# A state-space scan on one core: carries copied once for three units, delta and x multiplied after the transpose, and one scaling in eight moved to GpSimd

## The chip, the cores and the metric

The kernel runs on one core of one Trainium2 chip. The metric is device time in microseconds, from one execution to the next the median of three: 25196.08 us (25184.54 to 25197.58). A core has five engines that run side by side and meet only at semaphores: PE (TensorE, matrix multiplications and transposes into PSUM), DVE (VectorE), ACT (ScalarE), POOL (GpSimd) and SP, which here only issues DMAs. Each engine works through its own queue in order. An instruction that waits holds up everything behind it on its engine, and nothing elsewhere, unless something elsewhere needs it.

## What is computed

Two layers on 8 images of 64 x 64 tokens and 192 channels, in fp32. The change lies in the second, a selective scan in four directions `k` (rows, columns, and both backwards) over 384 inner channels and 16 states per channel:

```
xs     = silu(conv3x3(in_proj(x)))                 # in four orders of the tokens
dts, B, C = x_proj(xs);   delta = softplus(dt_proj(dts) + bias)
h[t]   = exp(delta[t] * A) * h[t-1] + (delta[t] * xs[t]) * B[t]      # per channel and state
y[t]   = sum over states of h[t] * C[t]
out    = out_proj(layernorm(y1 + y2 + y3 + y4 + xs*D) * silu(z)) + x
```

## The kernel before, in words

`layer1` handles one image after another. For each there are two parts. First a stage that I call the front: a planner (`Flow`) interleaves `front` (projection, 3x3 convolution and silu of image b, with its results stored in DRAM twice, by rows in `xo[0]` and by columns in `xo[1]`), `prologue` (what the first stretch of the scan needs) and `finish` (layer norm, gate and output projection of image b-1). The planner is a list of generators: each yields a step with its engine and an estimated cost, or takes and gives a slot of a pool; the step that can start first comes next. What it picks becomes a fixed order of instructions on each engine. Then comes `main`, the scan, whose order is written out by hand.

The scan of an image has 32 steps (4 directions x 8 stretches of 512 tokens). A step has 24 units: 8 pairs `p` of states times 3 groups `d` of 128 channels. A unit holds 2 halves `f` of 64 channels x 2 states on the 128 partitions, 512 tokens wide. For unit u, `main` emits in this order:

- `run(u)`: two `tensor_tensor_scan` on DVE (L1561), one for each half, then on POOL the copy of the last column to `cy`, the carry into the next step (L1573), and the product `hc` of h and C (L1575)
- `decay(u + 2)`: two exponentials on ACT (`ea`, L1534)
- `weigh`, 3, 3 and 2 times in the three units of a pair: on ACT, delta times x, laid out by tokens (`duT`), is scaled by a column of B (`pw`, L1519). Eight of these, 4 blocks `j` of tokens x 2 states `i`, make the input of one pair. The list `todo` runs ten ahead: the eighth scaling of pair p+1, (j=3, i=1), is emitted in the middle unit, 3p+1, of pair p
- `supply(u + 1)`: eight transposes on PE turn `pw` into `g` (L1545), the additive input of the scan, in PSUM with two buffers
- `collect(u - 1)`: PE sums `hc` over the states into `y` (L1590); `add(u - 2)`, for the last pair alone, adds y to the accumulator on DVE (L1601, L1599)
- one piece of `prepare(s + 1)`, from a table: loading xc, `project`, `keep`, `turn_b`, `step`, `soft` (three activations), `delta` on DVE (L1447), `times_u` (delta times x, on POOL, L1454), `turn` (PE, L1460), `keep_du` (copies the transposed product from PSUM to `duT`, DVE, L1467)

So the queues read: PE `supply(u+1), collect(u-1), supply(u+2), collect(u)`; POOL `cy(u), hc(u), cy(u+1), hc(u+1)`. Pools that matter: `hs` and `hc` 3 buffers each, `g` 2, `ea` 3, `pw` 8 tiles (two pairs).

Of the kernel before, what the change touches and what calls it, by code (L numbers as in the profile page):

```python
# [8 lines left out]
F32 = mybir.dt.float32  # L9
# [985 lines left out]
def layer1(tc, consts, x1s, mv1, out, w_in, w_x, w_dt, w_out):  # L995
# [7 lines left out]
    with ExitStack() as ctx:  # L1003
# [47 lines left out]
        nc.vector.tensor_copy(gb.rearrange("p m b -> p (m b)"), pb[:, : 2 * DT * nb])  # L1051

        wxz = [wp.tile([CP, CT, DIN], F32, name=f"wi1{n}") for n in "xz"]

        keeper = []
        o = lambda ins: keeper[-1](ins)

        def scaled(f, b, half):

            for ct in range(CT):  # L1060
                r = yield step(
                    "ACT",
                    0.6,
                    lambda: [
                        nc.scalar.activation(
                            wxz[half][:, ct],
                            wi[:, ct, half * DIN : half * DIN + DIN],
                            AF.Copy,
                            scale=sc[:, b * CT + ct : b * CT + ct + 1],
                        )  # L1070
                    ],
                )
            return r

        def front(f, cx, mq, b, xo):

            fp = cx.enter_context(tc.tile_pool(name="fr1", bufs=1, reuse_waits="tile"))
            pads = [fp.tile([128, HI + 2, WI + 2], F32, name=f"pad{i}") for i in range(2)]
            for tag, n in (("xl", 3), ("fx", 2), ("pad", 2), ("xs", 2), ("xt", 1)):
                f.pool(tag, n)  # L1080
            got = {}

            def load():
                for d in range(DT):
                    for t in range(NT):
                        tk = slice(t * TT, t * TT + TT)
                        yield "take", "xl"
                        xl = got["xl", d, t] = fp.tile([CP, CT, TT], F32, name="xl1", bufs=3)
                        r = yield step("SP", 0.1, lambda: [nc.sync.dma_start(out=xl, in_=image(x1s[b])[:, :, tk])])
                        f.at["xl", d, t] = r + 3  # L1090

            def project():
                yield from scaled(f, b, 0)
                for d in range(DT):
                    for t in range(NT):
                        yield "wait", ("xl", d, t)
                        xl = got["xl", d, t]
                        yield "take", "fx"
                        ps = got["ps", d, t] = mq.tile([128, TT], F32, name="p_x1", tag="fx", bufs=2)
                        r = f.at["ps", d, t] = yield step(  # L1100
                            "PE",
                            1.9,
                            lambda: [
                                nc.tensor.matmul(
                                    ps, wxz[0][:, ct, d * 128 : d * 128 + 128], xl[:, ct], start=ct == 0, stop=ct == 1
                                )
                                for ct in range(CT)
                            ],
                        )
                        f.give("xl", r)  # L1110
# [61 lines left out]
            def store():  # L1172
                for d in range(DT):
                    yield "wait", ("conv", d)
                    xs = got["xs", d]
                    for h in range(2):
# [11 lines left out]
                            r,  # L1188
                        )
                    yield "take", "xt"  # L1190
                    xt = fp.tile([128, WI, HI], F32, name="xt1")
                    r = yield step("ACT", 7.2, lambda: [nc.scalar.copy(xt, xs.rearrange("p h w -> p w h"))])
                    f.give("xs", r + 5)
                    r = yield step(
                        "SP", 0.1, lambda: [nc.sync.dma_start(out=xo[1][:, d], in_=xt.rearrange("p w h -> p (w h)"))], r
                    )
                    f.give("xt", r + 10)
                f.at["front"] = r

            return [convolve(), fill(), project(), load(), store()]  # L1200

        def finish(f, cx, mq, b):

            fp = cx.enter_context(tc.tile_pool(name="fi1", bufs=1, side="right", reuse_waits="tile"))
            full = [128, DT, TT]
            for tag, n in (("sq", 1), ("rs", 2), ("z", 2), ("xl2", 3)):
                f.pool(tag, n)
# [72 lines left out]
            def gate():  # L1280
                yield from scaled(f, b, 1)
                for t in range(NT):
                    yield "wait", ("xl2", t)
                    xl = got["xl2", t]
                    for d in range(DT):
# [6 lines left out]
                                nc.tensor.matmul(  # L1292
                                    ps, wxz[1][:, ct, d * 128 : d * 128 + 128], xl[:, ct], start=ct == 0, stop=ct == 1
                                )
# [71 lines left out]
        def scan(xo):  # L1366
# [18 lines left out]
            def prepare(s, bank=lambda name: mp.tile([128, TT], F32, name=name, tag="mm")):  # L1385
# [5 lines left out]
                def load():  # L1391
                    st["xc"] = pools["pr1"].tile([128, DT, TT], F32, name="xc")
                    o(nc.sync.dma_start(out=st["xc"], in_=xo[k % 2][:, :, c * TT : c * TT + TT]))
                    if first(s):
                        st["wd"] = pools["pr1"].tile([45, DIN], F32, name="wd")
# [55 lines left out]

                def times_u(d):
                    st["du", d] = pools["pr1"].tile([128, TT], F32, name="du", tag="tmp")
                    o(nc.gpsimd.tensor_mul(st["du", d], st["de", d], st["xc"][:, d]))  # L1454

                def turn(d):
                    st["p_du", d] = pt = bank("p_du")
                    for j in range(NB1):
                        o(
                            nc.tensor.transpose(  # L1460
                                pt[:, j * 128 : j * 128 + 128], st["du", d][:, j * 128 : j * 128 + 128], ident
                            )
                        )

                def keep_du(d):
                    o(
                        nc.vector.tensor_copy(  # L1467
                            st["duT"][:, :, d * 128 : d * 128 + 128],
                            st["p_du", d].rearrange("p (j t) -> p j t", j=NB1),
                        )  # L1470
                    )
# [10 lines left out]
                    9: [(delta, 0), (step, 1)],  # L1482
                    10: [(soft, 1), (times_u, 0)],
                    11: [(delta, 1), (turn, 0), (repeat_delta, s, 0)],
                    12: [(keep_du, 0), (step, 2), (times_u, 1)],
                    13: [(soft, 2)],
                    14: [(delta, 2), (turn, 1)],
                    15: [(keep_du, 1), (times_u, 2)],
                    16: [(turn, 2)],
# [22 lines left out]
            def weigh(s, p, j, i):  # L1512

                st = state[s]
                if i == 0:
                    st["pw", p, j] = pools["pw1"].tile([128, 2 * DT, 2, 64], F32, name="pw")
                n = 2 * p + i
                o(
                    nc.scalar.activation(  # L1519
                        st["pw", p, j][:, :, i],  # L1520
                        st["duT"][:, j].rearrange("p (g c) -> p g c", c=64),
                        AF.Copy,
                        scale=st["bt"][:, j, n : n + 1],
                    )
                )

# [25 lines left out]
            def run(u):  # L1552
# [3 lines left out]
                ea, g = made.pop(("e", u)), made.pop(("g", u))  # L1556
                h = pools["h1"].tile([128, 2, TT], F32, name="hs")
                rev = (lambda ap: ap) if k < 2 else (lambda ap: ap[:, ::-1])
                for f in range(2):
# [9 lines left out]
                    )  # L1569
                if "cy" not in st:  # L1570
                    st["cy"] = pools["pr1"].tile([128, NP1, DT, 2], F32, name="cy")
                last = TT - 1 if k < 2 else 0
                o(nc.gpsimd.tensor_copy(st["cy"][:, p, d], h[:, :, last]))  # L1573
                made["hc", u] = hc = pools["h1"].tile([128, 2, TT], F32, name="hc")
                o(nc.gpsimd.tensor_mul(hc, h, bc(st["cb", p], 1, [128, 2, TT])))  # L1575

            def collect(u):
# [30 lines left out]
            def prologue(f, mq, front_pools):  # L1608

                yield "wait", "front"  # L1610
                front_pools.close()
                for name, n in (("pr1", 2), ("dr1", 4), ("pw1", 8), ("bc1", 3), ("e1", 3)):
                    spool(name, n)
# [18 lines left out]
                for t in todo[:10]:  # L1632
                    yield step("ACT", 0.55, lambda: weigh(*t), f.free["ACT"])
                for u in range(2):
                    yield step("ACT", 1.35, lambda: decay(u), None, "explog")

            def prologue_of(f, d):
# [9 lines left out]
                yield step("SP", 0.1, lambda: repeat_delta(0, d), r)  # L1647
                yield "take", "tmp"
                r = yield step("POOL", 1.3, lambda: ready["times_u"](d), r)
                yield "take", "mm"  # L1650
                r = yield step("PE", 0.6, lambda: ready["turn"](d))
                f.give("tmp", r)
                yield "wait", "bt"
# [4 lines left out]
            def main():  # L1658
                for name, n, kw in (("h1", 3, {}), ("y1", 1, dict(space=PSUM)), ("g1", 2, dict(space=PSUM))):
                    spool(name, n, **kw)  # L1660
                supply(0)
                rest = iter(todo[10:])
# [32 lines left out]
        for b in range(nb + 1):  # L1695
# [8 lines left out]
            if b < nb:  # L1704
                xo = [ddp.tile([128, DT, L], F32, name=f"xo{i}") for i in range(2)]
                chains += front(f, fr_x, mq, b, xo)
                prologue, main = scan(xo)
# [112 lines left out]
```

## Time and profile before

| | us |
|---|---|
| median of three runs | 25196.08 |
| the profiled execution | 25213.53 |
| its span, first to last instruction | 25211.5 |
| layer 0, up to the first `hc` | 5863.9 |
| one image's scan, first to last of 768 `hc` (8297.7 to 10486.4) | 2188.7 |
| one front between two scans (last `hc` 8055.9 to first `hc` 8297.7) | 241.8 |

The profiled execution lies 17 us above the median. Times in the timeline count from the start of the span. A group's mean is the duration of one instruction; two of the same engine can overlap by a little, so what counts for the rate is the distance from start to start.

### The profile page before, as it was taken

Reading aid. Unit: us, or ns where it says so; the run is one execution under the profiler, and the core shown is the slowest. Engines: PE = TensorE matmul, PEld = TensorE weight load, DVE = VectorE, ACT = ScalarE, POOL = GpSimd, SP = SyncE. Lnnn points to the kernel's source line nnn. Section 1 sums busy time; section 2 is a strip of 40 time slices with the busy share of each in tenths; the row PEclk is TensorE's granted clock in tenths of the full one; section 3 lists DMA queues with packets and bytes.
Section 4 is the critical chain, followed back from the end, with each engine's and each line's share of the span. In section 5 each row is a group of like instructions: output and inputs, shape, how many; then the busy total and the mean of one; then the engine's idle time right before and its main releaser. Section 6 shows DMA issues by size and latency. Waiting matters only on the chain.

```text
span 25211.5 us, 312991 instructions
## 1 busy us (share of the span) xinstructions
PE 21347.4 (85%) x100012; PEld 10381.6 (41%) x100012; DVE 21583.5 (86%) x22090; ACT 21653.2 (86%) x38251; POOL 16862.8 (67%) x13639
## 2 busy tenths in 40 slices
PE   7888888887888888888888888888888888888888
PEld 3444444443443444344434443444344434443444
DVE  6777667658999899899989998999899989988998
ACT  5666566558998999899989998999899989998998
POOL 0111111116997799599959995999599959986997
PEclk7888888888999999999999999999999999999999
DMA  1111111112222222222222222222222222222222
GB/s 45 38 36 42 37 37 42 33 28 88 66 66 76 78 65 69 85 68 65 66 88 66 66 66 87 66 66 69 85 67 67 64 89 65 67 66 87 66 66 59
DMA packets 1129703, 1608.06 MB, mean 64 GB/s; under 512 B 259360, under 2 KB 458432, under 8 KB 1118848
## 3 DMA queue, kind: packets, MB, share of 16 engines
q1 hardware_dynamic: 1128064, 1588.03, 22.4%
q8 instruction: 806, 13.21, 0.2%
q14 instruction: 833, 6.82, 0.1%
HBM read 1024.65 MB, written 160.17 MB: 47 GB/s over the span
## 4 chain that ended last, share of the span: by engine, by line
POOL 55%; PE 23%; issue 9%; DVE 6%; ACT 4%; DMA 3%; SPq 1%; POOLq 0%; DVEq 0%; ACTq 0%
POOL hc L1575 49%; POOL cy L1573 4%; DVE xs L1165 3%; PE p_f L937 2%; PE y L1590 2%; PE p_x L429 2%; PE p_f L957 2%; PE p_z L512 2%; POOL du L1454 1%; DMA xc<-xo 1%; PE p_y L771 1%; DVE xs L325 1%; PE p_o L854 1%; PE p_o L1339 1%; PE p_y L768 1%
## 5 line engine op out<-in xcount | busy, mean ns | idle before, releaser
L1575 POOL TENSOR_TENSOR hc<-hs,cb 128x1024 f32<-128x1024 f32 x6144 | 14582.9, 2374 | 10.4 <-POOL cy L1573 6.1
L1561 DVE TENSOR_TENSOR_SCAN hs<-ea,cy,g 128x512 f32<-128x512 f32 x10752 | 13058.6, 1263 | 787.6 <-PE g L1545 425.4
L1519 ACT ACTIVATE pw<-duT,bt 128x384 f32<-128x384 f32 x16384 | 8873.2, 601 | 12.8 <-DVE duT L1467 12.8
L1590 PE MATMUL y<-hc,sel 128*64 128x512 f32 x24576 | 6655.0, 620 | 2467.4 <-POOL hc L1575 2461.7
L1534 ACT ACTIVATE ea<-dr,an 128x512 f32<-128x512 f32 x12288 | 8125.5, 709 | 348.9 <-DVE hs L1561 326.2
L1545 PEld LDWEIGHTS g<-ident,pw 128*128 128x128 f32 x49152 | 5306.8, 141 | 4303.0 <-issue 2670.4
L1545 PE MATMUL g<-ident,pw 128*128 128x128 f32 x49152 | 6773.8, 280 | 30.6 <-DVE hs L1561 12.9
L1590 PEld LDWEIGHTS y<-hc,sel 128*64 128x64 f32 x24576 | 1228.9, 135 | 3886.9 <-POOL hc L1575 3627.0
L1573 POOL COPY cy<-hs 128x2 f32<-128x2 f32 x6144 | 1165.1, 190 | 1547.2 <-DVE hs L1561 1482.2
L1454 POOL TENSOR_TENSOR du<-de,xc 128x512 f32<-128x512 f32 x768 | 983.4, 1280 | 1639.2 <-DVE de L1447 1621.1
L1561 DVE TENSOR_TENSOR_SCAN hs<-ea,g 128x512 f32<-128x512 f32 x1536 | 1776.9, 1204 | 178.1 <-PE g L1545 122.7
L346 POOL TENSOR_TENSOR s<-x 96x512 f32<-96x512 f32 x64 | 88.5, 1383 | 2366.9 <-DVE x L325 2169.7
L346 POOL TENSOR_TENSOR s<-sq 96x512 f32<-96x512 f32 x128 | 221.2, 1728 | 1049.2 <-ACT sq L359 909.8
L1433 PE MATMUL p_dt<-xdbl,wd 13*128 13x512 f32 x1536 | 857.3, 639 | 41.4 <-DVE de L1447 39.5
L1165 DVE SCALAR_TENSOR_TENSOR xs<-pad,p,xs 128x4096 f32<-128x4096 f32 x192 | 860.8, 4484 | 36.9 <-ACT xs L1155 29.7
L1404 PE MATMUL p_d<-xc,wx 128*44 128x512 f32 x1536 | 792.1, 598 | 96.3 <-DMA xc<-xo 96.3
L937 PE MATMUL p_f<-h,wf 96*128 96x512 f32 x1536 | 786.4, 656 | 4.8 <-ACT m L913 3.3
L325 DVE SCALAR_TENSOR_TENSOR x<-xx,p,x 96x512 f32<-96x512 f32 x1024 | 720.2, 744 | 29.3 <-ACT x L314 29.1
L1447 DVE SCALAR_TENSOR_TENSOR de<-p_dt,spa 128x512 f32<-128x512 f32 x768 | 524.0, 682 | 255.6 <-ACT spa L1442 253.4
L325 DVE SCALAR_TENSOR_TENSOR xs<-xin,p,xs 96x512 f32<-96x512 f32 x1024 | 702.0, 755 | 17.2 <-ACT xs L314 17.2
L957 PE MATMUL p_f<-m,wf 128*96 128x512 f32 x1536 | 711.3, 614 | 0.8 <-ACT m L913 0.8
L1601 DVE TENSOR_TENSOR yacc<-yacc,y 128x512 f32<-128x512 f32 x576 | 624.6, 1084 | 18.5 <-PE y L1590 18.5
(199 smaller groups left out, 20330.1 us busy)
## 6 DMA issues: line engine op xcount, KB each, us to landing
cb<-cd SPq DMA_DIRECT2D x4096, 128.0 KB
dr<-de SPq DMA_DIRECT2D x3072, 128.0 KB
xc<-xo SPq DMA_DIRECT2D x256, 768.0 KB
e<-csd SPq DMA_DIRECT2D x256, 384.0 KB
xl<-x SPq DMA_DIRECT2D x256, 384.0 KB
xo<-xs SPq DMA_DIRECT2D x48, 1024.0 KB
xo<-xt SPq DMA_DIRECT2D x24, 2048.0 KB
xl<-in_x SPq DMA_DIRECT2D x64, 384.0 KB
```

The costliest lines, as they stand in the source:

```text
L325: nc.vector.scalar_tensor_tensor(im(out[:, ct]), tap(ct, j), w[:, ct, j : j + 1], im(out[:, ct]), ALU.mult, ALU.add)
L937: nc.tensor.matmul(ps, wf1[:, ct, mt * 128 : mt * 128 + 128], h[:, ct], start=ct == 0, stop=ct == 1)
L957: nc.tensor.matmul(ps[:CP], wf2[:, kt, ct * CP : ct * CP + CP], m[:, kt], start=kt == 0, stop=kt == 5)
L1165: nc.vector.scalar_tensor_tensor(xs, tap(j), kw[:, d, j : j + 1], xs, ALU.mult, ALU.add)
L1454: o(nc.gpsimd.tensor_mul(st["du", d], st["de", d], st["xc"][:, d]))
L1519: nc.scalar.activation(st["pw", p, j][:, :, i], st["duT"][:, j].rearrange("p (g c) -> p g c", c=64), AF.Copy, scale=st["bt"][:, j, n : n + 1],
L1534: nc.scalar.activation(ea[:, f], state[s]["dr", d][:, f], AF.Exp, scale=an[:, k, p, at : at + 1])
L1545: nc.tensor.transpose(g[:, f, j * 128 : j * 128 + 128], state[s]["pw", p, j][:, 2 * d + f].rearrange("p a b -> p (a b)"), ident,)
L1561: nc.vector.tensor_tensor_scan(rev(h[:, f]), rev(ea[:, f]), rev(g[:, f]), 0.0 if first(s) else state[s - 1]["cy"][:, p, d, f : f + 1], ALU ...
L1573: o(nc.gpsimd.tensor_copy(st["cy"][:, p, d], h[:, :, last]))
L1575: o(nc.gpsimd.tensor_mul(hc, h, bc(st["cb", p], 1, [128, 2, TT])))
L1590: o(nc.tensor.matmul(y[half[f]], sel, hc[:, f], start=p == 0 and k > 0, stop=p == NP1 - 1))
```

## The change

Four edits that belong together:

1. The two `hs` tiles of a unit become one tile for the three units of a pair, with 2 buffers, and the carries of the pair are copied once, after the third `hc`: 8 copies of 128x6 in a step instead of 24 of 128x2. `hc` comes right after the scan, and has 2 buffers instead of 3.
2. `times_u` goes. `turn` transposes delta itself, and `keep_du` multiplies it by x, laid out by tokens (`ut`), on its way out of PSUM. For this the front stores x a third time, by tokens (`by_tokens`: transposes, an ACT copy and a DMA for each of 24 tiles), and each step loads `ut`, by one DMA or, for columns, two.
3. The eighth scaling of each pair, (j=3, i=1), runs on POOL.
4. To make room: the scaled projection weights move into the front's and the finish's own pools, `xl` has 2 buffers instead of 3, and the `ea` pool opens in `main`, so that `decay(0)` and `decay(1)` are emitted there and not in the planned part.

```diff
             def front(...):
+            wx_b = fp.tile([CP, CT, DIN], F32, name="wx1b")
-            for tag, n in (("xl", 3), ("fx", 2), ("pad", 2), ("xs", 2), ("xt", 1)):
+            for tag, n in (("xl", 2), ("fx", 2), ("pad", 2), ("xs", 2), ("xt", 1), ("xq", 2)):
...
+                        f.fork(by_tokens(d, h, xs, r))
...
+            def by_tokens(d, h, xs, r):
+                xf = xs.rearrange("p h w -> p (h w)")
+                for g in range(h * NT // 2, h * NT // 2 + NT // 2):
+                    yield "take", "fx"
+                    ps = mq.tile([128, TT], F32, name="p_xq", tag="fx", bufs=2)
+                    r = yield step("PE", 0.6, lambda: [nc.tensor.transpose(...) for j in range(NB1)], max(r, f.now))
+                    yield "take", "xq"
+                    xq = fp.tile([128, NB1, 128], F32, name="xq1", bufs=2)
+                    q = yield step("ACT", 0.6, lambda: [nc.scalar.copy(xq.rearrange("p j c -> p (j c)"), ps)], r)
+                    f.give("fx", q)
+                    dst = xo[2][g * TT : g * TT + TT, d * 128 : d * 128 + 128].rearrange("(j p) c -> p j c", p=128)
+                    q = yield step("SP", 0.1, lambda: [nc.sync.dma_start(out=dst, in_=xq)], q)
...
                 def load():
+                    st["ut"] = pools["pr1"].tile([128, NB1, DIN], F32, name="ut", bufs=1)
+                    if k % 2 == 0:
+                        o(nc.sync.dma_start(out=st["ut"], in_=src))
+                    else:
+                        for i in range(2): ...
...
-                def times_u(d):
-                    st["du", d] = pools["pr1"].tile([128, TT], F32, name="du", tag="tmp")
-                    o(nc.gpsimd.tensor_mul(st["du", d], st["de", d], st["xc"][:, d]))
...
                 def keep_du(d):
-                        nc.vector.tensor_copy(
+                        nc.vector.tensor_mul(
                             st["duT"][:, :, d * 128 : d * 128 + 128],
                             st["p_du", d].rearrange("p (j t) -> p j t", j=NB1),
+                            st["ut"][:, :, d * 128 : d * 128 + 128],
...
             def weigh(s, p, j, i):
+                if (j, i) == (NB1 - 1, 1):
+                    o(nc.gpsimd.tensor_scalar_mul(dst, src, scale))
+                else:
+                    o(nc.scalar.activation(dst, src, AF.Copy, scale=scale))
...
             def run(u):
-                h = pools["h1"].tile([128, 2, TT], F32, name="hs")
+                if d == 0:
+                    st["hs"] = pools["h1"].tile([128, DT, 2, TT], F32, name="hs")
+                h = st["hs"][:, d]
...
-                o(nc.gpsimd.tensor_copy(st["cy"][:, p, d], h[:, :, last]))
                 made["hc", u] = hc = pools["h1"].tile([128, 2, TT], F32, name="hc")
                 o(nc.gpsimd.tensor_mul(hc, h, bc(st["cb", p], 1, [128, 2, TT])))
+                if d == DT - 1:
+                    o(nc.gpsimd.tensor_copy(st["cy"][:, p], st["hs"][:, :, :, last]))
...
-                for name, n, kw in (("h1", 3, {}), ("y1", 1, dict(space=PSUM)), ("g1", 2, dict(space=PSUM))):
+                for name, n, kw in (("e1", 3, {}), ("h1", 2, {}), ("y1", 1, dict(space=PSUM)), ("g1", 2, dict(space=PSUM))):
+                decay(0)
+                decay(1)
                 supply(0)
```

More of the change, by code (lines that the diff above doesn't have):

```diff
@@ L1051, in layer1, with scaled @@
         nc.vector.tensor_copy(gb.rearrange("p m b -> p (m b)"), pb[:, : 2 * DT * nb])
-        wxz = [wp.tile([CP, CT, DIN], F32, name=f"wi1{n}") for n in "xz"]
         keeper = []
         o = lambda ins: keeper[-1](ins)
-        def scaled(f, b, half):
+        def scaled(w, b, half):
             for ct in range(CT):
@@ L1065, in scaled @@
                         nc.scalar.activation(
-                            wxz[half][:, ct],
+                            w[:, ct],
                             wi[:, ct, half * DIN : half * DIN + DIN],
@@ L1087, in load @@
                         yield "take", "xl"
-                        xl = got["xl", d, t] = fp.tile([CP, CT, TT], F32, name="xl1", bufs=3)
+                        xl = got["xl", d, t] = fp.tile([CP, CT, TT], F32, name="xl1", bufs=2)
                         r = yield step("SP", 0.1, lambda: [nc.sync.dma_start(out=xl, in_=image(x1s[b])[:, :, tk])])
@@ L1092, in project @@
             def project():
-                yield from scaled(f, b, 0)
+                yield from scaled(wx_b, b, 0)
                 for d in range(DT):
@@ L1104, in project @@
                                 nc.tensor.matmul(
-                                    ps, wxz[0][:, ct, d * 128 : d * 128 + 128], xl[:, ct], start=ct == 0, stop=ct == 1
+                                    ps, wx_b[:, ct, d * 128 : d * 128 + 128], xl[:, ct], start=ct == 0, stop=ct == 1
                                 )
@@ L1192, in store @@
                     r = yield step("ACT", 7.2, lambda: [nc.scalar.copy(xt, xs.rearrange("p h w -> p w h"))])
-                    f.give("xs", r + 5)
+                    if last := f.part(("xs", d), 3, r + 5):
+                        f.give("xs", last)
                     r = yield step(
@@ L1197, in store @@
                     f.give("xt", r + 10)
-                f.at["front"] = r
+                if last := f.part("front", 2 * DT + 1, r):
+                    f.at["front"] = last
+            def by_tokens(d, h, xs, r):
[3 more added lines that the diff above has]
+                    ps = mq.tile([128, TT], F32, name="p_xq", tag="fx", bufs=2)
+                    r = yield step(
+                        "PE",
+                        0.6,
+                        lambda: [
+                            nc.tensor.transpose(
+                                ps[:, j * 128 : j * 128 + 128], xf[:, g * TT + j * 128 : g * TT + j * 128 + 128], ident
+                            )
+                            for j in range(NB1)
+                        ],
+                        max(r, f.now),
+                    )
+                    yield "take", "xq"
[4 more added lines that the diff above has]
+                    q = yield step("SP", 0.1, lambda: [nc.sync.dma_start(out=dst, in_=xq)], q)
+                    f.give("xq", q + 2)
+                if last := f.part(("xs", d), 3, r):
+                    f.give("xs", last)
+                if last := f.part("front", 2 * DT + 1, q):
+                    f.at["front"] = last
             return [convolve(), fill(), project(), load(), store()]
@@ L1205, in finish @@
             full = [128, DT, TT]
+            wz_b = fp.tile([CP, CT, DIN], F32, name="wz1b")
             for tag, n in (("sq", 1), ("rs", 2), ("z", 2), ("xl2", 3)):
@@ L1280, in gate @@
             def gate():
-                yield from scaled(f, b, 1)
+                yield from scaled(wz_b, b, 1)
                 for t in range(NT):
@@ L1292, in gate @@
                                 nc.tensor.matmul(
-                                    ps, wxz[1][:, ct, d * 128 : d * 128 + 128], xl[:, ct], start=ct == 0, stop=ct == 1
+                                    ps, wz_b[:, ct, d * 128 : d * 128 + 128], xl[:, ct], start=ct == 0, stop=ct == 1
                                 )
@@ L1393, in load @@
                     o(nc.sync.dma_start(out=st["xc"], in_=xo[k % 2][:, :, c * TT : c * TT + TT]))
+                    st["ut"] = pools["pr1"].tile([128, NB1, DIN], F32, name="ut", bufs=1)
+                    if k % 2 == 0:
+                        src = xo[2][c * TT : c * TT + TT].rearrange("(j p) m -> p j m", p=128)
+                        o(nc.sync.dma_start(out=st["ut"], in_=src))
+                    else:
+                        for i in range(2):
+                            src = xo[2].rearrange("(h w) m -> w h m", w=WI)[c * RT + i : c * RT + RT : 2]
+                            o(nc.sync.dma_start(out=st["ut"][i * 64 : i * 64 + 64], in_=src.rearrange("j h m -> h j m")))
                     if first(s):
@@ L1460, in turn @@
                             nc.tensor.transpose(
-                                pt[:, j * 128 : j * 128 + 128], st["du", d][:, j * 128 : j * 128 + 128], ident
+                                pt[:, j * 128 : j * 128 + 128], st["de", d][:, j * 128 : j * 128 + 128], ident
                             )
@@ L1482, in prepare @@
                     9: [(delta, 0), (step, 1)],
-                    10: [(soft, 1), (times_u, 0)],
+                    10: [(soft, 1)],
                     11: [(delta, 1), (turn, 0), (repeat_delta, s, 0)],
-                    12: [(keep_du, 0), (step, 2), (times_u, 1)],
+                    12: [(keep_du, 0), (step, 2)],
                     13: [(soft, 2)],
                     14: [(delta, 2), (turn, 1)],
-                    15: [(keep_du, 1), (times_u, 2)],
+                    15: [(keep_du, 1)],
                     16: [(turn, 2)],
@@ L1517, in weigh @@
                 n = 2 * p + i
[L1518 to L1525, printed above, removed]
+                dst, src = st["pw", p, j][:, :, i], st["duT"][:, j].rearrange("p (g c) -> p g c", c=64)
+                scale = st["bt"][:, j, n : n + 1]
+                if (j, i) == (NB1 - 1, 1):
+                    o(nc.gpsimd.tensor_scalar_mul(dst, src, scale))
+                else:
+                    o(nc.scalar.activation(dst, src, AF.Copy, scale=scale))
             def decay(u):
@@ L1569, in run @@
                     )
[L1570 to L1573, printed above, removed]
                 made["hc", u] = hc = pools["h1"].tile([128, 2, TT], F32, name="hc")
                 o(nc.gpsimd.tensor_mul(hc, h, bc(st["cb", p], 1, [128, 2, TT])))
+                if d == DT - 1:
+                    if "cy" not in st:
+                        st["cy"] = pools["pr1"].tile([128, NP1, DT, 2], F32, name="cy")
+                    last = TT - 1 if k < 2 else 0
+                    o(nc.gpsimd.tensor_copy(st["cy"][:, p], st["hs"][:, :, :, last]))
             def collect(u):
@@ L1611, in prologue @@
                 front_pools.close()
-                for name, n in (("pr1", 2), ("dr1", 4), ("pw1", 8), ("bc1", 3), ("e1", 3)):
+                for name, n in (("pr1", 2), ("dr1", 4), ("pw1", 8), ("bc1", 3)):
                     spool(name, n)
@@ L1632, in prologue @@
                 for t in todo[:10]:
-                    yield step("ACT", 0.55, lambda: weigh(*t), f.free["ACT"])
-                for u in range(2):
-                    yield step("ACT", 1.35, lambda: decay(u), None, "explog")
+                    if t[2:] == (NB1 - 1, 1):
+                        yield step("POOL", 0.8, lambda: weigh(*t), 0.0)
+                    else:
+                        yield step("ACT", 0.55, lambda: weigh(*t), f.free["ACT"])
             def prologue_of(f, d):
@@ L1647, in prologue_of @@
                 yield step("SP", 0.1, lambda: repeat_delta(0, d), r)
-                yield "take", "tmp"
-                r = yield step("POOL", 1.3, lambda: ready["times_u"](d), r)
                 yield "take", "mm"
-                r = yield step("PE", 0.6, lambda: ready["turn"](d))
-                f.give("tmp", r)
+                yield step("PE", 0.6, lambda: ready["turn"](d), r)
                 yield "wait", "bt"
@@ L1705, in layer1 @@
                 xo = [ddp.tile([128, DT, L], F32, name=f"xo{i}") for i in range(2)]
+                xo.append(ddp.tile([L, DIN], F32, name="xo2"))
                 chains += front(f, fr_x, mq, b, xo)
```

## The prediction

> **What bounds the kernel now.** I read the page first: the busy shares and the chain of work that ended last.
>
> ```profile
> PE 21347.4 (85%) x100012; PEld 10381.6 (41%) x100012; DVE 21583.5 (86%) x22090; ACT 21653.2 (86%) x38251; POOL 16862.8 (67%) x13639
> ...
> POOL hc L1575 49%; POOL cy L1573 4%; DVE xs L1165 3%; PE p_f L937 2%; PE y L1590 2%; PE p_x L429 2%; PE p_f L957 2%; PE p_z L512 2%; POOL du L1454 1%; DMA xc<-xo 1%; PE p_y L771 1%; DVE xs L325 1%; PE p_o L854 1%; PE p_o L1339 1%; PE p_y L768 1%
> ```
>
> The chain names POOL, and all three POOL instructions that the change removes or thins out stand in it. Shares over a whole span mix stages, so I took the scan of one image alone, cut by direction (columns: PE, PEld, DVE, ACT, POOL, clock, DMA share, GB/s).
>
> ```profile
> 8300.00:8840.00 540.00, 476.42 (x2584) 231.10 (x2584) 497.30 (x464) 529.14 (x953) 498.44 (x403) 1.00 0.24 65
> 8850.00:9390.00 540.00, 452.56 (x2463) 222.53 (x2462) 504.61 (x460) 525.72 (x944) 492.33 (x399) 1.00 0.23 64
> 9400.00:9940.00 540.00, 461.68 (x2516) 227.01 (x2514) 505.18 (x471) 535.31 (x964) 504.74 (x407) 1.00 0.24 66
> ```
>
> Here ACT is busy 97 to 99% of the time, DVE 92 to 94%, POOL 91 to 93%: three engines in balance. 768 products from 8297.7 to 10486.4 us make 2188.7 / 767 = 2.854 us for a unit, 68.5 us for a step of 24, 8.56 us for a pair of states. Where engines balance, latencies decide, so the third view is the timeline of one image's scan.
>
> ```profile
> 10003.65 0.24 POOL L1573 COPY cy<-hs 128x2 f32<-128x2 f32 x1
> 10003.77 1.61 ACT L1519 ACTIVATE pw<-duT,bt 128x384 f32<-128x384 f32 x3
> ...
> 10004.83 1.38 PE L1545 MATMUL g<-ident,pw 128*128 128x128 f32 x8
> ...
> 10005.43 0.53 PEld L1545 LDWEIGHTS g<-ident,pw 128*128 128x128 f32 x5 [0.30 <-ACT pw L1519]
> ...
> 10014.15 7.12 DVE L1561 TENSOR_TENSOR_SCAN hs<-ea,cy,g 128x512 f32<-128x512 f32 x6
> ```
>
> and, from the step before:
>
> ```profile
> 9760.50 1.09 PE L1545 MATMUL g<-ident,pw 128*128 128x128 f32 x8
> ...
> 9761.73 2.45 DVE L1561 TENSOR_TENSOR_SCAN hs<-ea,cy,g 128x512 f32<-128x512 f32 x2 [1.14 <-PE g L1545]
> ...
> 9764.25 0.19 POOL L1573 COPY cy<-hs 128x2 f32<-128x2 f32 x1 [0.94 <-DVE hs L1561]
> ```
>
> Four latencies come out of this. The last scaling of a pair ends at 10003.77 + 1.61 = 10005.38; PE had stopped at the fourth block's transpose, does five more and ends at 10004.83 + 1.38 = 10006.21: 0.83 us from scaling to g. g ended at 9761.59 and the scan that waited began at 9761.73: 0.14. That scan ended at 9764.18 and POOL began at 9764.25: 0.07. Six scans in a row take 7.12, so a unit of two takes 2.38 from start to start, 2.45 to its end. The same timeline has an `hc` at 10001.34 and the next POOL instruction at 10003.65: 2.31 from start to start.
>
> **What the Trainium skill says.** "GPSIMD Engine Reference", section "Elementwise — side-by-side cycle accounting": an operation with two tensor inputs has a floor of about 2.5 cycles an element, since both reads share a port; its section "Engine selection" says that one-input operations run at roughly line rate. The trace agrees: `hc` has 1024 elements in 2374 ns and `du` 512 in 1280, so 2.14 ns an element and 186 ns fixed, while a copy of 132 elements takes 290 ns and one of 2 takes 190, 0.8 ns an element.
>
> ```profile
> L877 POOL COPY xx<-xx x56: 284/290/7972, 236.8 to 5534.7; 96x132 f32<-96x132 f32 x56
> ```
>
> "ScalarE: Activation LUTs", section "What ACT_TABLE_LOAD costs": 186 ns plus 93 for a per-partition operand plus 0.833 an element, and neighbours overlap by 93. That is 599 ns for a scaling (the row of L1519 has 601), and three take 1.61, so one more costs 0.505.
>
> **The change part by part, for a step.**
>
> ACT loses 8 of 64 scalings, 8 x 0.505 = 4.0 us. It ran at 97 to 99% of 68.5, so it can do a step in some 63.5 and bounds nothing any more.
>
> POOL loses three `du` (3 x 1.28 = 3.8) and 16 of 24 carry copies (16 x 0.14, the distance 10003.65 to the `hc` behind it, = 2.2), and gains 8 scalings of W each. No row has a per-partition scaling of 128x384 on POOL. From below: the copies' rate, 186 + 384 x 0.8 = 0.49 us; from above: a two-input product, 186 + 384 x 2.14 = 1.01. It reads one tensor, but also a scalar a partition, and writes in six strided rows; I take 0.62, nearer the low end, and keep both for the range. So POOL needs about as much as before (-6.0 + 5.0) and isn't full either.
>
> DVE: `keep_du` becomes a product from PSUM, about 0.69 (the row `xx<-p_o,xs` has 686 ns) instead of 0.67: nothing. By load alone DVE would be the next bound: 24 x 2.38 = 57.1, plus per step three `delta` and three `keep_du` (4.1), `keep` and `keep_b` (0.85) and three adds at 0.67 by rows or 1.28 by columns: 64 to 66 us.
>
> The new wait is what decides. The eighth scaling of pair p+1 is emitted after `run(3p+1)`, so in POOL's queue it stands behind `hc(3p+1)`, which cannot begin before the scan of unit 3p+1 has ended. `supply(3p+3)` needs it for its fourth transpose, and the scan of unit 3p+3 needs all eight. ACT, without that product ahead of it, delivered it early. This makes a loop over one pair: scan 3p+1, its product, the scaling, five transposes, scan 3p+3, and one more scan to 3p+4, where the next round begins:
>
> 2.45 (scan) + 0.07 + 2.31 (hc) + 0.62 (scaling) + 0.83 (PE) + 0.14 + 2.38 (scan 3p+3) = 8.80 us.
>
> Eight pairs: 70.4 a step, already over 68.5. Behind the waiting transpose stand `collect(3p+1)` and `supply(3p+4)` on PE; by the loop's times these end 1.09 + 1.0 after the fifth transpose, in time for scan 3p+4 (2.38 after 3p+3), except where a piece lies between: `project(0)` in unit 2 (1.02) costs 0.7 once a step, and in the first direction the skip matmuls another 1.1. DVE's extra work hides in the stall when it falls behind scans 3p+1 or 3p+2, since scan 3p+3 waits 1.6 us there; what follows a scan of unit 3p+3 does not: `delta(0)` in unit 9, `keep_du(0)` in 12, `keep_du(1)` in 15, and one add of three, 0.68 + 0.69 + 0.69 + 0.67 to 1.28, on average 3.0. Step: 70.4 + 3.0 + 0.7 + 0.3 (1.1 in a quarter of the steps) = 74.4, against 68.5: +5.9. Times 256 steps: +1510 us.
>
> The other buffers cost nothing by this count: `hc` with 2 needs `collect(u-2)`, which ends before scan u does; `hs` for a pair is asked for again six units later.
>
> Front: 24 ACT copies of a 128x512 bank, at some 0.5 each start to start, and 24 x 4 transposes (0.65 each four, as `p_du` at 10042.90) mostly lie beside the convolution, where DVE is the bound (117 of 120 us busy) and ACT idles half the time. Bare is the tail: after the last silu another 8 copies and 2 MB stored ahead of the load of xc, which took 9.96 us behind the xt store already, while `du` leaves the prologue's chain (1.3). SP issues all of these in order. I take +6 an image, from 0 to 20, in all +50. `decay(0)` and `decay(1)` in `main` are hidden: ACT was free at 8289 and the first scan waited for g until 8295.07. The `ut` loads (768 KB a step, one or two issues) have some 12 units before `keep_du(0)` wants them, and the DMA engines are 24% busy.
>
> Sum, against the profiled execution: 25213.5 + 1510 + 50 = 26774; the median lies 17 lower, and part of today's stalls at pair ends is counted in both sums, so I round down to 26,700.
>
> **Rivals.** (1) Slower, but by POOL's own price: W near 1.0, as a two-input product, adds 0.39 x 2048 pairs = 800: 27,500. For it: the strided output. Against it: the copies. (2) The wait is largely the one that is there already: ACT's scaling comes late today too (g waited for pw 984 us in all), so a pair grows only by 0.2: +410 + 50, 25,650. (3) The other side, faster: the wait does not bind, ACT's 4 us are the gain, and DVE decides with 65 us a step and about 2 of today's stalls, 67: -1.5 x 256, 24,850. For it: ACT's 99%, and a POOL queue shorter by 1 us. It needs the scaling to end within 2.38 - 0.97 = 1.4 us of scan 3p+1's end, where the product in front of it takes 2.31; so it holds only if the scaling did not stand behind that product, or if the scan needed only half of g, and the scan that waited began after the eighth transpose.
>
> **Chances.** The forecast 0.60, rival 1 0.14, rival 2 0.13, rival 3 0.11, no change 0.02. My range, 25,600 to 27,500, takes in rival 2 and the upper price of W and leaves out rival 3 and a little above. A measurement of this kernel tells 0.2% from no change. Slower: 0.60 + 0.14 + 0.13 = 0.87.
>
> **What would show it.** Right: in the waits, PE's weight load of g waiting for POOL's pw, about 1.5 us in 2048 pairs, and DVE's scans waiting for g, far above today's 548; ACT and DVE down to 86 to 88% in the scan; 73 to 75 us a step. The POOL scaling's row gives W. Wrong: ACT or DVE still above 95%, or the scan's wait ending on ea; a front longer than 260 us would put the loss elsewhere.

## The result, and the profile after

The changed kernel takes 29407.43 us (29380.3 to 29446.31) against 25192.64 for the kernel before (four executions each): the ratio is 1.1675, with a 95% interval of 1.1654 to 1.1695. Slower, as forecast, but 2,700 us more than the 26,700 predicted and outside the range. The profiled execution has a span of 29378.6 us. Its page, shares and granted clock of PE:

```profile
PE 23739.5 (81%) x100780; PEld 11405.7 (39%) x100780; DVE 21668.7 (74%) x22090; ACT 21217.7 (72%) x36402; POOL 17927.8 (61%) x10823
...
PEclk7888888898889888988898889888888898889888
...
L1607 POOL TENSOR_TENSOR hc<-hs,cb 128x1024 f32<-128x1024 f32 x6144 | 14535.4, 2369 | 4591.0 <-PE g L1579 1456.1
L1597 DVE TENSOR_TENSOR_SCAN hs<-ea,cy,g 128x512 f32<-128x512 f32 x10752 | 13061.9, 1264 | 4508.9 <-PE g L1579 2619.7
...
L1557 POOL TENSOR_SCALAR pw<-duT,bt 128x384 f32<-128x384 f32 x2048 | 2563.5, 1252 | 1754.6 <-DVE duT L1502 1338.2
```

The same two kinds of line on the page of before:

```profile
PEclk7888888888999999999999999999999999999999
...
L1561 DVE TENSOR_TENSOR_SCAN hs<-ea,cy,g 128x512 f32<-128x512 f32 x10752 | 13058.6, 1263 | 787.6 <-PE g L1545 425.4
```

DVE and ACT do about as many microseconds of work as before, and the products `hc` take no longer; what is new is the idle time in front of the scans, 4508.9 us instead of 787.6. The POOL scaling has a row of its own: 1252 ns. PE's clock line shows mostly 8 in the scan where the page of before has 9. The waits of the changed kernel name the place (us in total, times, longest; PEld is PE's weight load, and `issue` is time in which nothing that the profile shows was waited for):

```profile
ACT ea L1568 <- DVE hs L1597: 4736.8, 3577, 7.0
PEld g L1579 <- POOL pw L1557: 4376.3, 2040, 3.4
PE g L1579 <- POOL pw L1557: 3892.5, 2040, 3.2
PEld g L1579 <- issue: 3689.3, 3560, 2.8
DVE hs L1597 <- PE g L1579: 3077.7, 2646, 3.3
```

PE's transposes wait for POOL's scaling 2040 times; there are 2048 pairs of states. The scans wait for those transposes, and ACT for buffers that the scans free. The same stretch as the windows of before, in the third image:

```profile
9360.00:9900.00 540.00, 427.16 (x1997) 205.60 (x1995) 411.13 (x373) 411.02 (x713) 426.48 (x253) 0.87 0.25 66
```

No engine is above 80% busy, where ACT had 97 to 99. One round of the loop in the timeline, with two bursts of PE work from before and after it:

```profile
7308.80 1.87 PE L1579 MATMUL g<-ident,pw 128*128 128x128 f32 x8
...
7310.70 2.45 DVE L1597 TENSOR_TENSOR_SCAN hs<-ea,cy,g 128x512 f32<-128x512 f32 x2 [0.53 <-PE g L1579]
...
7313.33 2.37 POOL L1607 TENSOR_TENSOR hc<-hs,cb 128x1024 f32<-128x1024 f32 x1 [1.14 <-DVE hs L1597]
...
7313.68 1.08 PE L1627 MATMUL y<-hc,sel 128*64 128x512 f32 x4
...
7314.69 0.55 PE L1579 MATMUL g<-ident,pw 128*128 128x128 f32 x3
7315.68 1.24 POOL L1557 TENSOR_SCALAR pw<-duT,bt 128x384 f32<-128x384 f32 x1
...
7316.97 0.77 PE L1579 MATMUL g<-ident,pw 128*128 128x128 f32 x5 [1.74 <-POOL pw L1557]
...
7317.83 2.45 DVE L1597 TENSOR_TENSOR_SCAN hs<-ea,cy,g 128x512 f32<-128x512 f32 x2 [0.94 <-POOL pw L1557]
...
7327.90 1.98 PE L1627 MATMUL y<-hc,sel 128*64 128x512 f32 x4
```

The loop begins in the second line: the scan ends at 7313.15, the product begins 0.18 later, the scaling 2.35 after that, and ends at 7316.92; three transposes had long been made, the other five start at 7316.97, and the scan begins at 7317.83. From scan to scan over two units this is 7.13 us, where two units at DVE's own pace take 4.7.

The first and the last line are PE at about half speed: the eight transposes take 1.87 where the prediction's line at 9760.50 has 1.09, the four sums into y 1.98 where the line at 7313.68 has 1.08. No term of the prediction had this. The clock record of the traces knows only two values, full and half, in stretches that are almost all multiples of 3.41 us. From 5,900 us to the end the kernel before has 77 stretches at half speed, 440 us in all; the changed kernel has 1,259, 5,539 us.

The front between two scans went from 241.8 to 249.6 us (last `hc` of one image 8553.8, first of the next 8803.4), 8 an image against the 6 predicted. The scan carries the rest.

### The profile page after: what moved, and what is told of

The parts are those of the page before. It is cut to its first block, busy times and chain, and to the rows that moved or that the text cites. A ratio compares the mean times of both kernels' runs of the same rounds, so it can differ in the third digit from the quotient of the medians.

```text
span 29378.6 us, 313320 instructions
## 1 busy us (share of the span) xinstructions
PE 23739.5 (81%) x100780; PEld 11405.7 (39%) x100780; DVE 21668.7 (74%) x22090; ACT 21217.7 (72%) x36402; POOL 17927.8 (61%) x10823
## 5 line engine op out<-in xcount | busy, mean ns | idle before, releaser
L1597 DVE TENSOR_TENSOR_SCAN hs<-ea,cy,g 128x512 f32<-128x512 f32 x10752 | 13061.9, 1264 | 4508.9 <-PE g L1579 2619.7
L1579 PE MATMUL g<-ident,pw 128*128 128x128 f32 x49152 | 8078.8, 307 | 3909.9 <-POOL pw L1557 3892.5
L1579 PEld LDWEIGHTS g<-ident,pw 128*128 128x128 f32 x49152 | 6030.0, 156 | 9375.6 <-POOL pw L1557 4376.3
L1627 PE MATMUL y<-hc,sel 128*64 128x512 f32 x24576 | 7713.3, 710 | 574.5 <-POOL hc L1607 566.8
L1559 ACT ACTIVATE pw<-duT,bt 128x384 f32<-128x384 f32 x14336 | 7829.4, 600 | 5.2 <-DVE duT L1502 3.6
L1557 POOL TENSOR_SCALAR pw<-duT,bt 128x384 f32<-128x384 f32 x2048 | 2563.5, 1252 | 1754.6 <-DVE duT L1502 1338.2
L1627 PEld LDWEIGHTS y<-hc,sel 128*64 128x64 f32 x24576 | 1363.5, 150 | 1962.5 <-issue 1140.3
L1443 PE MATMUL p_d<-xc,wx 128*44 128x512 f32 x1536 | 917.3, 684 | 19.3 <-DMA xc<-xo 19.3
L1495 PEld LDWEIGHTS p_du<-ident,de 128*128 128x128 f32 x3072 | 367.1, 156 | 735.1 <-issue 533.3
L1479 ACT ACTIVATE spa<-p_dt 128x512 f32<-128x512 f32 x768 | 453.6, 591 | 257.1 <-PE p_dt L1472 239.2
```

The source lines that it names most:

```text
L1443: nc.tensor.matmul(st["p_d"][:44], wx[:, d, k], st["xc"][:, d], start=d == 0, stop=d == DT - 1)
L1557: o(nc.gpsimd.tensor_scalar_mul(dst, src, scale))
L1559: o(nc.scalar.activation(dst, src, AF.Copy, scale=scale))
L1579: nc.tensor.transpose(g[:, f, j * 128 : j * 128 + 128], state[s]["pw", p, j][:, 2 * d + f].rearrange("p a b -> p (a b)"), ident,)
L1597: nc.vector.tensor_tensor_scan(rev(h[:, f]), rev(ea[:, f]), rev(g[:, f]), 0.0 if first(s) else state[s - 1]["cy"][:, p, d, f : f + 1], ALU ...
L1627: o(nc.tensor.matmul(y[half[f]], sel, hc[:, f], start=p == 0 and k > 0, stop=p == NP1 - 1))
```

## Experiments

Theory 1: the loop through the POOL scaling, by its place in the queue, is the whole loss in the scan. Rivals: other edits share it, or POOL's load does. The planner emits the first ten scalings of an image; where an edit changes which scaling runs on POOL, it does so there too, in lines that are not printed below.

**All scalings on ACT again.**

```diff
-                if (j, i) == (NB1 - 1, 1):
-                    o(nc.gpsimd.tensor_scalar_mul(dst, src, scale))
-                else:
-                    o(nc.scalar.activation(dst, src, AF.Copy, scale=scale))
+                o(nc.scalar.activation(dst, src, AF.Copy, scale=scale))
```

> The changed kernel with all eight scalings on ACT again; carries, product at the eviction and token layout stay. Theory 1 (the POOL scaling behind hc is the whole loss in the scan): the loop over a pair is gone, ACT is the bound again at 67 to 68 us a step, fronts stay 8 us longer: 24,950 to 25,400 us, clock back at 0.95. Rival (two hc buffers, the hs tile of three units or the late carry bring their own wait): 26,000 us or more, with POOL hc waiting for PE y still above 1000 us.

Measured: 25160.16 us, ratio 0.9989 (0.998 to 0.9998), clock 0.955. ACT is the bound again, 98% in the windows of its scan:

```profile
8830.00:9370.00 540.00, 459.09 (x2485) 223.65 (x2484) 505.64 (x463) 528.14 (x950) 452.13 (x251) 1.00 0.29 77
```

The other three edits together are worth nothing or 0.1%: an image's scan takes 2178.2 us instead of 2188.7 (first `hc` 8273.4, last 10451.6), and the longer front takes most of that back. The rival about buffers falls for a kernel without the POOL scaling.

**The kernel before with this scaling alone on POOL.** In its `weigh` the two branches of the changed kernel, nothing else:

```diff
+                if (j, i) == (NB1 - 1, 1):
+                    o(nc.gpsimd.tensor_scalar_mul(dst, src, scale))
+                else:
+                    o(nc.scalar.activation(dst, src, AF.Copy, scale=scale))
```

> The kernel before with only the scaling (j=3, i=1) on POOL, behind hc. Theory 1: the same loop as in the changed kernel, with du still on POOL: 29,000 to 29,900 us, PE g waiting for POOL pw in some 2040 pairs. Rival (the other edits carry part of the loss): below 28,000 us.

Measured: 29887.12 us, ratio 1.1868 (1.185 to 1.1886). The one edit alone makes the whole loss, and 480 us more; `du` and the single carries are still in POOL's queue there, which may be the reason. The wait is the same one:

```profile
PEld g L1543 <- POOL pw L1521: 4722.4, 2040, 3.4
```

**The same POOL work, asked for earlier.**

```diff
-                if (j, i) == (NB1 - 1, 1):
+                if (j, i) == (0, 1):
```

> The changed kernel with the scaling (j=0, i=1) on POOL instead of (j=3, i=1): as much work on POOL, but issued in unit 3p+2 for pair p+2, a whole pair before its transposes. Theory 1 (it is the place in the queue, not the load): the wait of g for pw goes; POOL carries 24 x 2.34 + 8 x 1.22 + 8 x 0.15 = 67 us a step and is close to the bound: 25,000 to 25,900 us. Rival (POOL's load, or what its tensor-scalar does to its neighbours): 27,500 us or more.

Measured: 25530.18 us, ratio 1.014 (1.0124 to 1.0155). The instruction is as long as before, and the row of its waiters shows that PE hardly waits for it, 1 and 1 times instead of 2040:

```profile
L1557 POOL TENSOR_SCALAR pw<-duT,bt x2048: 1233/1249/2678, 5870.1 to 25399.8; 128x384 f32<-128x384 f32 x187
...
  PEld g L1579: 2.6, 1
  PE g L1579: 2.2, 1
```

So 3,880 of the 4,215 us belong to the place in the queue, with what it does to PE's clock. POOL's load is a candidate for the remaining 1.4%, since POOL stands at 96% (519.59 of 540 us) in a window of this run's scan; this is not shown, and the run below with half as many speaks against load alone.

**A shorter instruction in the same place.** A copy leaves one of eight columns of B out of the product.

```diff
-                    o(nc.gpsimd.tensor_scalar_mul(dst, src, scale))
+                    o(nc.gpsimd.tensor_copy(dst, src))
```

> The changed kernel with the POOL scaling replaced by a copy of the same tiles in the same place, so that one of eight columns of B is left out of the product: only the duration of that one instruction changes. Theory 1 (loop of one pair, slope 1 in that duration): the copy takes 0.49 us, 0.76 less than the scaling, times 2048 pairs = 1560 us, and some of the slow clock of PE goes too: 27,000 to 27,900 us. Rival (the stall of PE and its clock decide, not the duration): 28,500 us or more.

Measured: 26994.24 us, ratio 1.0719 (1.0703 to 1.0735), clock 0.927. The copy takes 0.51 us:

```profile
L1557 POOL COPY pw<-duT x2048: 493/507/1969, 5865.2 to 26850.1; 128x384 f32<-128x384 f32 x187
```

0.74 us less in each of 2048 pairs, 1516 us, bring back 2413: 1.6 us for each us of duration. The loop alone gives a slope of 1; something else grows with the wait.

**PE kept busy while it waits.** Theory 2: what the loop costs beyond that slope is PE's clock. `supply` of the first unit of a pair makes its first three transposes again, five times, into the same places, ahead of the one that waits for POOL; the inside of that loop stays as it is.

```diff
+                again = [(0, j) for j in range(NB1 - 1)] * 5 if d == 0 else []
+                order = [(0, j) for j in range(NB1 - 1)] + again + [(0, NB1 - 1)] + [(1, j) for j in range(NB1)]
-                for f in range(2):
-                    for j in range(NB1):
+                for f, j in order:
```

> The changed kernel with 15 more transposes in front of the one that waits for POOL in each pair: the first three blocks again, into the same places, some 1.75 us of PE work where PE stood still for 1.9 us. Theory 2 (what the loop costs beyond the scaling's duration is PE's lower clock after the idle stretch): the granted clock rises from 0.87 to 0.95 or more, the five transposes after the scaling fall from 1.05 to 0.83 us and the next units by 0.35: some 0.57 us in 2048 pairs, 28,000 to 28,700 us. Rival (the clock is a mere companion, or the added work delays PE as much): 29,200 us or more.

Measured: 28318.1 us, ratio 1.1239 (1.1221 to 1.1256): 1,089 us less than the changed kernel, with 30,720 more transposes. The granted clock is 0.956 instead of 0.873, 1.00 in the scan, with 92 stretches at half speed left of 1,259. A sum into y takes 617 ns in the mean instead of 710; it was 620 in the kernel before.

```profile
9360.00:9900.00 540.00, 478.83 (x2940) 279.91 (x2938) 435.82 (x397) 439.94 (x765) 453.30 (x269) 1.00 0.24 65
```

The starts of the scans in the two traces tell where the clock costs its time. From scan 3p+1 to 3p+3, the stretch with the wait and the five transposes, the mean is 7.37 us in the changed kernel and 7.30 here; from 3p+3 to 3p+4, where the next sums and transposes of PE have to keep up, it is 3.22 and 2.76.

**A third length in the same place.**

```diff
-                    o(nc.gpsimd.tensor_scalar_mul(dst, src, scale))
+                    o(nc.gpsimd.tensor_mul(dst, src, scale.unsqueeze(2).to_broadcast([128, 2 * DT, 64])))
```

> The changed kernel, the scaling in its place (j=3, i=1) behind hc, but as the product of two tensors that took 0.83 us. Copy and tensor-scalar operation in that place gave 26,994 us at 0.51 and 29,407 us at 1.25: 1.6 us a pair for each us of duration. If the loss is proportional to the duration, 28,040 us (27,700 to 28,300); if the added part is PE's clock and that falls only past some length of the wait, the point lies under the line, at slope 1 from the copy: 27,650 us or less, with the clock still at 0.92 or more.

Measured: 27994.65 us, ratio 1.1116 (1.11 to 1.1131), clock 0.91, the product at 0.83 us. On the line: 0.51, 0.83 and 1.25 us give 26,994, 27,995 and 29,407, and the clock falls along with it, 0.927, 0.91, 0.873. There is no step between these lengths.

**What the operation costs.** Two kernels with the early place, where PE hardly waits for it: the product of two tensors above, and a tensor-scalar operation with the constant 1.0 (which leaves one of eight columns of B out).

```diff
-                    o(nc.gpsimd.tensor_scalar_mul(dst, src, scale))
+                    o(nc.gpsimd.tensor_scalar_mul(dst, src, 1.0))
```

> As the run with (j=0, i=1) on POOL, but as a product of two tensors, the scalar broadcast along the row, instead of a tensor-scalar operation. If a per-partition scalar is what makes the tensor-scalar operation dear, the product takes 186 + 384 x 2.14 = 1.0 us, POOL has 65 us a step, and the time is 25,000 to 25,300 us; if the strided rows of the output are dear, it takes 1.25 us or more and the time is 25,500 us.

> As the run with (j=0, i=1) on POOL, with an immediate 1.0 as the scalar, so that one of eight columns of B is left out of the product: it prices the operation. If reading the per-partition scalar costs, the operation falls from 1.25 us to the copy's 0.51; if the tensor-scalar operation itself is slow, it stays at 1.1 to 1.25 us.

```profile
L1557 POOL TENSOR_TENSOR pw<-duT,bt x2048: 815/829/2272, 5834.8 to 24960.1; 128x384 f32<-128x384 f32 x187
```

```profile
L1557 POOL TENSOR_SCALAR pw<-duT x2048: 1159/1174/2608, 5861.9 to 25304.9; 128x384 f32<-128x384 f32 x187
```

The first is the product, the second the constant. All have the same shapes and strided rows as the scaling. So neither the rows (the product and the copy have them too) nor the per-partition scalar (0.08 us) is dear, but the tensor-scalar operation of this engine itself: 1.25 and 1.17 against 0.83 for two inputs and 0.51 for a copy. The early product gives 25145.85 us, ratio 0.9978 (0.997 to 0.9986); the constant, in one run, 25456.29.

**Fewer of them.** The early place for every other pair only, first as the tensor-scalar operation (its edit, against the run with the early place), then as the product, under the same condition.

```diff
-                if (j, i) == (0, 1):
+                if (j, i) == (0, 1) and p % 2 == 0:
```

> As the run with (j=0, i=1) on POOL, but only for every other pair: 4 of 64 scalings of a step. Theory 1: by load ACT needs 67.5 - 2.0 = 65.5 us a step, POOL 57.4 + 4 x 1.22 = 62.3, DVE 64 to 66 plus some 2 of stalls: 66.5 to 67.5 us a step against 68.5, that is 24,700 to 25,000 us, faster than both kernels. Rival (DVE's own stalls at 68 to 69 us set the step whatever ACT does): 25,100 to 25,250 us.

> As the run with the early product of two tensors, for every other pair only: POOL 57.4 + 4 x 0.8 = 60.6 us a step, ACT 65.5. If a POOL instruction between two hc costs by its length where hc, the sum on PE and the transposes just keep pace with the scans, half as many cost half as much: 25,020 to 25,130 us, under the 25,146 of all eight. If ACT's load decides (65.5 against 63.5), slower than that: 25,150 to 25,250 us.

Measured: 25299.15 us, ratio 1.0046 (1.0034 to 1.0059), outside both of its ranges, and 25106.48, ratio 0.9971 (0.996 to 0.9982). With ACT at 95% and POOL at 90% in a window of the first (511.22 and 485.81 of 540), load does not explain its time: even an early, half as frequent tensor-scalar operation costs more than ACT gains. That `hc`, the sum and the transposes have no slack against the scans is argued from the latencies, not shown. The second is the fastest of all, though its interval overlaps that of the early product for every pair.

## Why the prediction was right in its mechanism and wrong in its size

The loop is as predicted: its place, its order (scan, product, scaling, five transposes, scan), the pairs that wait, the engines behind it that fall idle. The same edit alone shows the loss, and the same work earlier does not. What failed is the size of the loop: the scaling's cost W was taken at half of what it is, and what the wait does to PE's clock was put at nothing. The front was off by 2 us an image. The other edits (buffers, late carry, the product in `keep_du`) were put at nothing and cost nothing with all scalings on ACT. In the changed kernel itself `hc` waits for the sums on PE 914 times, 1439.5 us in all; with PE kept busy it is 148 times, 183.1 us. So most of these waits come with the slow clock; what they cost by themselves was not measured.

Three terms were mis-sized and one was missing. The sum before rounding was 26774 - 17 = 26,757 us.

- **W, the scaling: 0.62 us taken, 1.25 measured.** (1.25 - 0.62) x 2048 = 1,290 us. I had bounded it by the copy's rate from below and a two-input product's from above. "GPSIMD Engine Reference", section "Engine selection", puts one-input operations at roughly line rate; the copy does that (0.51), this operation does not. The upper bound was no bound: the operation takes 1.5 times the product's 0.83. (For that product's floor the section that the prediction names has about 2.6 cycles an element; its 2.5 stands in the page's section "Instruction dispatch". The product with a broadcast scalar lies under the 2.14 ns an element of `hc`: (829 - 186) / 384 = 1.67.)
- **Latencies of the loop.** The product starts 0.18 after the scan and not 0.07, which was the carry copy's start. With 2.35 to the next POOL instruction instead of 2.31 the timeline above makes (0.11 + 0.04) x 2048 = some 300 us.
- **DVE's pace.** 2.38 was a third of the 7.12 us for three units, but the last of them counts with its full 2.45: from start to start it is (7.12 - 2.45) / 2 = 2.34. That takes 0.04 x 2048 = some 80 us off.
- **PE's clock, which had no term.** The run that keeps PE busy puts it at 1,089 us. "TensorE: Matmul & The Clock Gate", section "Part 1: The HAM clock gate", says that activity holds the clock up and that an idle window of about 3.4 us brings it to half. The trace agrees with the half (1.08 and 1.98) and with stretches of 3.41 us, but not with a whole idle window: the waits before it are mostly shorter, 1.9 us in the mean and 3.2 at most, and from 5,900 us on PE stood still for more than 3.4 us only 26 times against 1,259 stretches at half speed. I had read that the PE clock was 1.00 in the scan, and didn't ask what an idle PE would do to it.

26,757 + 1,290 + 300 - 80 + 1,089 = some 29,360, against 29,407. With PE kept busy the loop's own arithmetic holds: 2.45 + 0.18 + 2.35 + 1.25 + 0.83 + 0.14 + 2.34 = 9.54 a pair, 76.3 a step, and 4.0 for the rest as predicted, 80.3 us; measured, 28318 - 25192 = 3,126 over 256 steps, less 8 us a front, is 12.0 above 68.5, 80.5. Of the 4.0 only the sum is confirmed, not its single terms.

Rival 1 had the right suspicion, a dearer W, with a ceiling too low. Rival 3 named its own condition, that the scaling does not stand behind the product. The early place comes close to it, since there the scaling has a whole pair to spare; the kernel took 25,530 us, and 25,146 with the shorter product, but not 24,850. Why ACT's saved time brings so little then stays open.

## What to carry to other kernels

Before work moves to an engine with time to spare, write down what stands ahead of it in that queue, and when its reader asks for it: here the kernel took 17% longer than the one before with the instruction behind a product that waits for a scan, and 1.4% longer with the like of it asked for a whole pair earlier. Price each operation by a row of its own kind; a range between two other kinds is no bound. And where a new wait leaves PE idle in every round, add a term for its clock: here it was a quarter of the loss, 1,089 of 4,215 us.

## What the runs showed of the hardware

On POOL, for 128x384 fp32 with rows of 64: a copy 0.51 us, a product with a broadcast operand 0.83, a tensor-scalar product with a constant 1.17, with a per-partition scalar 1.25. Why the tensor-scalar product is slower stays open. Multiplying by a broadcast scalar as a second tensor takes a third less time here than the tensor-scalar operation. And PE's granted clock fell from 0.952 to 0.927, 0.91 and 0.873 as its waits grew with the lengths 0.51, 0.83 and 1.25, by stretches at half speed though hardly a wait was as long as 3.4 us. It was 0.956 when repeated transposes filled the wait, and the kernel was 1,089 us faster for it.
